# Neighbour words of consecutive nodes, and a block-wide merge in place of the second drain

## The chip, the cores and the metric

The kernel runs on one core of a Trainium2 chip. The metric is device microseconds of that core, as the median of 3 runs. The engines are TensorE (PE in the profile), VectorE (DVE), ScalarE (ACT), GpSimd (POOL) and SyncE (SP), which works off its queue of DMAs here. GpSimd issues all indirect DMAs: gathers and scatters by index.

## The reference

Two layers of a graph network over 4096 nodes with 128 features. The first is attention with 8 heads over the neighbours of each node, the second takes three quantiles, feature by feature, over the kept neighbours. Cut to what matters:

```python
adj = bernoulli(0.0078125, (4096, 4096)); adj = adj | adj.T | eye   # int32
# layer 0
Wh = einsum('nd,hde->hne', nodes, W)
e = leaky_relu(f1[:, :, None] + f2[:, None, :], 0.2)
att = softmax(where(adj > 0, e, -9e15), axis=-1)
h = elu(einsum('hnm,hmd->hnd', att, Wh))
x = layernorm(nodes + elu(cat(h) @ W1 + b1))
# layer 1
mask = adj != 0
keep = mask & ~remove      # remove: one or two neighbours, by rank in the row
svals = sort(where(keep[:, :, None], x[None], big), axis=1)
agg = mean of svals at the 0.25, 0.5 and 0.75 quantile of the kept
out = (0.5 * agg + 0.5 * x) @ W.T + b + x
```

A node has 64.6 neighbours on average, 98 at most.

## The kernel before

Nodes are worked in 32 tiles of 128, a node per partition. The kernel never uses the dense 4096 x 4096 matrix for the layers themselves. A front part (class `Front`) turns each row of adj into a list of up to 104 (`C1`) neighbour numbers, in descending order, -1 or less where there is none. From the lists, `place` finds each node's place among the nodes of its block, ordered by number of neighbours, and scatters the lists there (`rows_d`, line 543, on GpSimd's queue); `keep` makes the shorter list for the second layer. The attention part (`gat`) then gathers the neighbours' rows from DRAM with indirect DMAs (line 975, tile nb). After that comes `sparse`, the second layer, which begins when the first is done.

The tiles are cut into six blocks (`BLOCKS` = 4, 4, 6, 6, 6, 6). `Front.pieces` makes a list of pieces of work: for each block its first drains, second steps, second drains, `place`, and the `keep` of the block before. `gat` works on half tiles, u from 0 to 63. In each step it issues the gathers of half tile u+3 (`load`), multiplies half tile u on TensorE (`rows_sum`: spread, line 1107, on VectorE, then the matmuls into ps_z, line 1115), makes the softmax of u+1 (`probabilities`), copies ps_z out on ScalarE (`collect`, line 1130), moves older tiles on (`combine`), and then takes some pieces of front work:

```python
advance(3 if u < 2 * START[2] else 2)
```

`load` of the first half tile of a block calls `through(b)`, which works off all pieces up to that block's `place`. The row buffers nb are six tiles of 18 gathered rows. A scheduler sets the order of instructions on each engine; each engine works its own in order.

How a list is made, for one tile:

- `scan` loads four quarters of the adj rows (a_i, line 380, on SP's queue). ScalarE makes 0 and 1 in bf16 (nz): once with Relu of the negated value, which sums up negative entries (line 382), once with sign (line 389). TensorE adds 16 column stretches, weighted with 1, 2, 4 ... 2^15 (line 391). The result is 256 words of 16 bits in PSUM (ps_words). Word g holds the nodes g, g + 256, g + 512 and so on. A scan takes two tiles (the first two only one each), in four chunks, with two nz buffers of one chunk.
- `first` makes keys of word times 256 plus g (line 404) and takes the 104 largest by 13 rounds of `drain8`: MAX8 (line 190), and between rounds MATCH_REPLACE8 (line 192), which strikes the eight found ones out.
- `second`, for 2 to 4 tiles at once (`BATCH`), takes the highest bit of each word (`decode`, `peel`) into a candidate number, then drains words with a second bit (24, `C2`), and those with a third (8, `C3`), which are peeled six times (`PEELS`). This leaves 104 + 24 + 48 = 176 candidates in no order (cand).
- `last_` drains the 176 candidates again in 13 rounds into the list, sorted.

Tests that a limit was overflowed go into `spill`; if one was, a flag at the end of the first layer sends the program to a dense version (`general`).

Of the kernel before, what the change touches and what calls it, by code (L numbers as in the profile page):

```python
# [38 lines left out]
F32 = mybir.dt.float32  # L39
# [11 lines left out]
P = 128  # L51
# [19 lines left out]
C3 = 8  # L71
PEELS = 6
CAND = C1 + C2 + C3 * PEELS
# [28 lines left out]
BATCH = 4  # L102
# [83 lines left out]
def drain8(nc, out, work, rounds, gone):  # L186

    for r in range(rounds):
        top = out[:, ts(r, 8)]
        nc.vector.max(out=top, in_=work)  # L190
        if r < rounds - 1:
            nc.vector.match_replace(  # L192
                out=work, in_to_replace=top, in_values=work, imm_value=gone
            )


def peel(nc, pool, wf, base, ids, rest, tag):


    shape = list(wf.shape)  # L200
    e = ids.bitcast(I32)
    nc.vector.tensor_scalar(
        e,
        wf.bitcast(I32),
        23,
        NG1.bit_length() - 1,
        op0=ALU.logical_shift_right,
        op1=ALU.logical_shift_left,
    )
    if rest is not None:  # L210
        pw = pool.tile(shape, I32, name=f"pw_{tag}")
        nc.vector.tensor_scalar(pw, wf.bitcast(I32), 0x7F800000, None, op0=ALU.bitwise_and)
        nc.vector.tensor_sub(rest, wf, pw.bitcast(F32))
    nc.vector.tensor_tensor(ids, e, base, op=ALU.add)


def decode(nc, pool, keys, tag):

    shape = list(keys.shape)
    ki = pool.tile(shape, I32, name=f"ki_{tag}")  # L220
    nc.vector.tensor_copy(ki, keys)
    wi = pool.tile(shape, I32, name=f"wi_{tag}")
    nc.vector.tensor_scalar(wi, ki, NG1.bit_length() - 1, None, op0=ALU.logical_shift_right)
    nc.vector.tensor_scalar(ki, ki, NG1 - 1, None, op0=ALU.bitwise_and)
    wf = pool.tile(shape, F32, name=f"wf_{tag}")
    nc.vector.tensor_copy(wf, wi)
    base = pool.tile(shape, F32, name=f"base_{tag}")
    nc.vector.tensor_scalar(base, ki, -127.0 * NG1, None, op0=ALU.add)
    return wf, base
# [90 lines left out]
class Front:  # L320
# [3 lines left out]
    def __init__(self, tc, nc, c, adj, meta_d, ctx):  # L324
# [11 lines left out]
        self.iota_s = self.iota_g[:, :C1]  # L336
        self.pows = one.tile([P, WBITS, P], BF, name="pows")
# [18 lines left out]
        self.spill = one.tile([P, NT, 5], F32, name="spill")  # L356
# [11 lines left out]
        self.words, self.lists, self.counts = {}, {}, {}  # L368
        self.placed = None

    def scan(self, t, m):

        nc = self.nc
        ps_w = self.psum_w.tile([P, 2, NG1], F32, name="ps_words")
        quarter = N // 4
        for i in range(4):
            nz = self.tp.tile([P, 2, quarter], BF, name="nz", bufs=2)
            for j in range(m):
                a_i = self.tp.tile([P, quarter], I32, name="a_i", bufs=3)
                nc.sync.dma_start(out=a_i, in_=self.adj[ts(t + j, P), ts(i, quarter)])  # L380
                k = 4 * (t + j) + i
                nc.scalar.activation(  # L382
                    nz[:, j, :],
                    a_i,
                    AF.Relu,
                    scale=-1.0,
                    accum_out=self.negative[:, k : k + 1],
                )
                nc.scalar.sign(nz[:, j, :], a_i)
            for b in range(4):  # L390
                nc.tensor.matmul(
                    ps_w[:, :m, :],
                    self.pows[:, 4 * i + b, :],
                    nz[:, :m, ts(b, NG1)],
                    start=i + b == 0,
                    stop=i + b == 6,
                )
        for j in range(m):
            self.words[t + j] = ps_w[:, j, :]

    def first(self, t, k1):
        nc = self.nc
        key = self.tp.tile([P, NG1], F32, name="key")
        nc.vector.scalar_tensor_tensor(
            key, self.words.pop(t), float(NG1), self.iota_g, op0=ALU.mult, op1=ALU.add
        )
        drain8(nc, k1, key, C1 // 8, -1.0)

    def second(self, t, m, k1, cand):

        nc, one = self.nc, self.one
        k1, cand = k1[:, :m], cand[:, :m]
        sp = self.spill[:, t : t + m, :]
        wf, base = decode(nc, one, k1, f"1_{m}")
        rest = one.tile([P, m, C1], F32, name=f"rest1_{m}")
        peel(nc, one, wf, base, cand[:, :, :C1], rest, f"1_{m}")
        nc.vector.tensor_scalar(
            sp[:, :, 0:1], k1[:, :, C1 - 1 :], float(NG1), None, op0=ALU.is_ge
        )
        nc.vector.tensor_scalar(base, base, 127.0 * NG1, None, op0=ALU.add)  # L420
        nc.vector.scalar_tensor_tensor(rest, rest, float(NG1), base, op0=ALU.mult, op1=ALU.add)
        k2 = one.tile([P, m, C2], F32, name=f"k2_{m}")
        for j in range(m):
            drain8(nc, k2[:, j, :], rest[:, j, :], C2 // 8, -1.0)
        nc.vector.tensor_scalar(
            sp[:, :, 1:2], k2[:, :, C2 - 1 :], float(NG1), None, op0=ALU.is_ge
        )
        wf, base = decode(nc, one, k2, f"2_{m}")
        rest = one.tile([P, m, C2], F32, name=f"rest2_{m}")
        peel(nc, one, wf, base, cand[:, :, C1 : C1 + C2], rest, f"2_{m}")  # L430
        nc.vector.tensor_scalar(base, base, 127.0 * NG1, None, op0=ALU.add)
        nc.vector.scalar_tensor_tensor(rest, rest, float(NG1), base, op0=ALU.mult, op1=ALU.add)
        k3 = one.tile([P, m, C3], F32, name=f"k3_{m}")
        for j in range(m):
            drain8(nc, k3[:, j, :], rest[:, j, :], 1, -1.0)
        nc.vector.tensor_scalar(
            sp[:, :, 2:3], k3[:, :, C3 - 1 :], float(NG1), None, op0=ALU.is_ge
        )
        wf, base = decode(nc, one, k3, f"3_{m}")
        for r in range(PEELS):  # L440
            nxt = one.tile([P, m, C3], F32, name=f"rest3_{m}", bufs=2)
            at = C1 + C2 + C3 * r
            peel(nc, one, wf, base, cand[:, :, at : at + C3], nxt, f"3_{m}")
            wf = nxt
        left = one.tile([P, m], F32, name=f"left_{m}")
        nc.vector.reduce_sum(left, wf, axis=AX.X)
        nc.vector.tensor_scalar(sp[:, :, 3:4], left.unsqueeze(2), 0.0, None, op0=ALU.is_gt)

    def place(self, b):
# [5 lines left out]
        work = one.tile([P, max(BLOCKS), C1], F32, name="work")[:, :n, :]  # L455
# [116 lines left out]
    def keep(self, b):  # L572
# [7 lines left out]
        work = one.tile([P, max(BLOCKS), C1], F32, name="work")[:, :n, :]  # L580
# [125 lines left out]
    def pieces(self, order_d, flag_d):  # L706
# [10 lines left out]
        for b, n in enumerate(BLOCKS):  # L717
            lists = self.tp.tile([P, max(BLOCKS), C1], F32, name="lists")

            def open_(b=b, lists=lists):  # L720
                self.lists[b] = lists

            out.append(("open", open_))
            at = START[b]
            while at < START[b] + n:
                m = min(BATCH, START[b] + n - at)
                if n % BATCH:
                    m = n // -(-n // BATCH)
                bufs = {}

                def start(bufs=bufs):
# [1615 lines left out]
```

## Time and profile before

| | |
|---|---|
| median of 3 runs | 7530.93 us |
| lowest, highest | 7525.32, 7533.52 us |
| profiled execution, span | 8384.6 us |
| instructions in it | 31455 |
| granted TensorE clock, mean | 0.547 |
| first gather of the attention part | 142 us |
| 30th of 64 copies out of ps_z | 2219 us |
| last gathers of the attention part | about 3800 us |

The profiled execution's own time is its span of 8384.6 us, 854 us more than the median of the runs; all durations below are from that one execution. A row of a group has the line, engine and operation, output and input tiles, shapes, count, busy time, mean ns of one, and the idle time of that engine just before, with what ended it. "issue" is waiting that the profile puts down to nothing; "remote" is a wait whose release it does not show. One line of the code can stand for several uses, as line 190 for all drains; tile names tell them apart (k from key: first drain; k from rest: the short drains; lists from cand: second drain).

### The profile page before, as it was taken

The numbers are of one execution on the slowest core, as the hardware profiler recorded it, in microseconds if no ns is written. First come the engines' busy times: TensorE is split into PE (matmuls) and PEld (weight loads), VectorE is DVE, ScalarE is ACT, GpSimd is POOL, SyncE is SP. The second block draws the span as 40 slices with busy tenths as digits, with TensorE's granted clock in tenths as the row PEclk, the third lists the DMA queues.
The fourth block names the chain that finished last, engine by engine and source line by source line (L and its number), as shares of the span: only waits on it lengthen the run. The fifth ranks groups of instructions, "written<-read, shape, count | busy, mean of one in ns | idle before, by whom it ended". The sixth has DMA issues, their size and how long they took to land. (4 is left out here: it accounts for less than half of the span.)

```text
span 8384.6 us, 31455 instructions
## 1 busy us (share of the span) xinstructions
PE 1235.7 (15%) x6047; PEld 1032.2 (12%) x6047; DVE 5886.7 (70%) x9454; ACT 2218.9 (26%) x2338; POOL 4358.1 (52%) x4524
## 2 busy tenths in 40 slices
PE   2122222222332332330000000000000000000000
PEld 1121212222231322230000000000000000000000
DVE  6454564454222222224899999999999999999899
ACT  5021121000000000002344443443443433333333
POOL 3545546656666666666455456445554545354410
PEclk5565656565565666565555555555555555555555
DMA  6122222112112111111011111111111111011100
GB/s 192 43 89 71 74 77 64 49 38 50 50 48 50 50 49 50 50 41 39 26 36 35 33 36 43 31 32 38 34 34 31 38 30 35 27 34 32 31 9 1
DMA packets 219060, 380.98 MB, mean 45 GB/s; under 512 B 129283, under 2 KB 129412, under 8 KB 218852
## 3 DMA queue, kind: packets, MB, share of 16 engines
q0 software_dynamic: 145808, 308.58, 13.9%
q1 hardware_dynamic: 72898, 70.23, 2.8%
q14 instruction: 159, 1.30, 0.1%
q8 instruction: 49, 0.80, 0.0%
q10 hardware_dynamic: 146, 0.07, 0.0%
HBM read 368.26 MB, written 10.31 MB: 45 GB/s over the span
## 5 line engine op out<-in xcount | busy, mean ns | idle before, releaser
L1771 DVE TENSOR_TENSOR rows<-low,rows 128x2048 f32<-128x2048 f32 (+10 forms) x1970 | 3649.3, 1893 | 88.0 <-ACT low L1764 61.7
L1726 POOL DMA_INDIRECT rows<-x_d,info x2078 | 2031.9, 978 | 1863.7 <-ACT picked L1826 1184.2
L975 POOL DMA_INDIRECT nb<-xf_d,ids x2190 | 2078.1, 949 | 1329.5 <-issue 625.3
L1764 ACT COPY low<-rows 128x2048 f32<-128x2048 f32 (+8 forms) x985 | 1528.4, 1557 | 2331.8 <-DVE rows L1771 1665.3
L1115 PE MATMUL ps_z<-spread,nb 128*128 128x128 f32 x4500 | 757.9, 325 | 1491.4 <-issue 737.3
L1107 DVE TENSOR_TENSOR spread<-e,ps_small 128x1152 f32<-128x1152 f32 (+4 forms) x312 | 342.2, 1109 | 804.1 <-remote 594.0
L1115 PEld LDWEIGHTS ps_z<-spread,nb 128*128 128x128 f32 x4500 | 702.4, 237 | 1565.9 <-issue 996.7
L1833 PE MATMUL low<-sixth_i,picked 128*128 128x128 f32 x300 | 74.3, 430 | 4347.7 <-ACT low L1764 3413.6
L1833 PEld LDWEIGHTS low<-sixth_i,picked 128*128 128x128 f32 x300 | 65.0, 322 | 4357.0 <-ACT low L1764 3420.9
L1771 DVE TENSOR_TENSOR rows<-low_s,rows 128x512 f32<-128x512 f32 (+3 forms) x798 | 395.3, 523 | 128.7 <-remote 39.9
L1077 ACT ACTIVATE ps_e<-e 128x256 f32<-128x256 f32 (+4 forms) x64 | 26.1, 408 | 1513.9 <-DVE e L1067 556.2
L190 DVE MAX8 k<-key 128x8 f32<-128x256 f32 x416 | 169.0, 416 | 169.6 <-remote 119.5
L1764 ACT COPY low_s<-rows 128x512 f32<-128x512 f32 (+3 forms) x399 | 179.8, 486 | 281.6 <-DVE rows L1771 172.0
L1873 POOL DMA_INDIRECT out<-o,info x32 | 34.9, 1091 | 397.2 <-ACT o L1869 369.3
L1130 ACT COPY zT<-ps_z 128x512 f32<-128x512 f32 x64 | 37.6, 587 | 742.7 <-remote 586.0
L382 ACT ACTIVATE nz<-a_i 128x1024 bf16<-128x1024 int32 x128 | 134.2, 1049 | 328.9 <-remote 198.6
L190 DVE MAX8 lists<-cand 128x8 f32<-128x176 f32 x416 | 128.1, 332 | 69.7 <-remote 47.1
L192 DVE MATCH_REPLACE8 key<-k,key 128x256 f32<-128x256 f32 x384 | 156.1, 408 | 0.0
L1058 DVE TENSOR_TENSOR e<-nb,ps_small 128x64 f32<-128x64 f32 (+9 forms) x200 | 45.2, 237 | 154.4 <-DMA nb<-xf_d,ids 129.9
L1438 DVE SCALAR_TENSOR_TENSOR zT<-zT,ps_h 128x512 f32<-128x512 f32 x64 | 42.0, 682 | 158.0 <-ACT zT L1437 109.7
L1146 PE MATMUL ps_h<-zT,w_ga 128*128 128x256 f32 x256 | 105.3, 569 | 271.3 <-DVE s L1438 157.2
L1775 DVE TENSOR_TENSOR rows<-rows 128x256 f32<-128x256 f32 (+8 forms) x245 | 142.5, 583 | 1.6 <-DVE rows L1771 1.4
(245 smaller groups left out, 2429.0 us busy)
## 6 DMA issues: line engine op xcount, KB each, us to landing
a_i<-in_adj SPq DMA_DIRECT2D x128, 512.0 KB
nb<-xf_d,ids POOLq DMA_INDIRECT x2190
rows<-x_d,info POOLq DMA_INDIRECT x2078
xf_d<-xf POOLq DMA_DIRECT2D x4, 576.0 KB
xf<-in_x POOLq DMA_DIRECT2D x4, 512.0 KB
meta_d<-rowdata_k SPq DMA_DIRECT2D x4, 324.0 KB
abc_ta<-in_L_gnn_a POOLq DMA_DIRECT2D x2, 512.0 KB
w_ga<-in_L_gnn_W POOLq DMA_DIRECT2D x2, 512.0 KB
```

What stands on the lines that cost most here:

```text
L190: nc.vector.max(out=top, in_=work)
L192: nc.vector.match_replace(out=work, in_to_replace=top, in_values=work, imm_value=gone)
L382: nc.scalar.activation(nz[:, j, :], a_i, AF.Relu, scale=-1.0, accum_out=self.negative[:, k : k + 1],)
L975: gather = nc.gpsimd.indirect_dma_start(out=rows[:, used + i, :], out_offset=None, in_=xf_d, in_offset=bass.IndirectOffsetOnAxis(ap=ids[:, ...
L1107: last = nc.vector.tensor_tensor(spread[:, :m], e[:, at : at + m, :].unsqueeze(2).to_broadcast(shape), own.unsqueeze(1).unsqueeze(3).to_br ...
L1115: product = nc.tensor.matmul(ps_z[:, g, :], rows[:, k, :D], spread[:, i].rearrange("p j h -> p (j h)"), start=i0 + i == 0, stop=i0 + i == ...
L1146: nc.tensor.matmul(ps_h[:, k, :], w_sb[:, h0 + k, :], zT[:, h0 + k, :], start=True, stop=True)
L1726: return nc.gpsimd.indirect_dma_start(out=row, out_offset=None, in_=x1_d, in_offset=bass.IndirectOffsetOnAxis(ap=info[:, col : col + 1], a ...
L1764: nc.scalar.copy(packed, lows)
L1771: done = nc.vector.tensor_tensor(to, packed, highs, op=op)
L1775: nc.vector.tensor_tensor(lows, lows, highs, op=ALU.min)
L1833: product = nc.tensor.matmul(made["ps"], v, to, start=i == 0, stop=i == len(found))
```

## The change

A word now holds 16 consecutive nodes, so that the order of words is the order of nodes. The first drain takes keys that are largest for the highest group with a bit in it (group number times 65536 plus the word), 88 at most, in 11 rounds. The highest bit of each, one after the other, is a sorted list already. What is left of words with two or more bits (extras: 24 second bits, 8 words peeled five times) is drained to 24 sorted numbers, and these are merged into the sorted list in a bitonic merge of 128 places, for all tiles of a block in one instruction per half step. The second drain of every tile is gone. To get consecutive nodes, ScalarE writes nz transposed: each quarter is read in order and written with one bit position after the other, 128 elements apart; a scan has two chunks of twice the size, with 32 matmuls of half as many columns. `second` is cut into four pieces per block; `gat` takes 2 and later 1 piece per half tile.

```diff
+WORDS = 88
+PEELS = 5
+EXTRAS = 24
+MERGE = 128
-BATCH = 4
...
     def scan(self, t, m):
...
-        for i in range(4):
-            nz = self.tp.tile([P, 2, quarter], BF, name="nz", bufs=2)
+        for i in range(2):
+            nz = self.tp.tile([P, 2, WBITS, 2 * part], BF, name="nz", bufs=2)
             for j in range(m):
...
+                for q in range(2):
...
+                    to = nz[:, j, :, ts(q, part)].rearrange("p b g -> p g b")
+                    groups = a_i.rearrange("p (g b) -> p g b", b=WBITS)
+                    nc.scalar.activation(
+                        to,
+                        groups,
...
+                    nc.scalar.sign(to, groups)
+            for b in range(WBITS):
                 nc.tensor.matmul(
+                    ps_w[:, :m, ts(i, 2 * part)],
+                    self.pows[:, b, :],
+                    nz[:, :m, b, :],
...
     def first(self, t, k1):
...
+            key, words, 0.0, self.high, op0=ALU.is_gt, op1=ALU.mult
         )
-        drain8(nc, k1, key, C1 // 8, -1.0)
+        nc.vector.tensor_add(key, key, words)
+        drain8(nc, [k1[:, ts(r, 8)] for r in range(WORDS // 8)], key, 0.0)
...
+    def second(self, b, part):
...
+        if part == 3:
+            k4 = one.tile([P, most, EXTRAS], F32, name="k4")[:, :n]
+            for j in range(n):
+                tops = [k4[:, j, ts(r, 8)] for r in reversed(range(EXTRAS // 8))]
+                drain8(nc, tops, self.extra[:, j], -1.0e6)
...
+            for i in range(8):
+                nc.vector.tensor_copy(w[:, :, :, i], v[:, :, :, 7 - i])
+            self.merge(b, up)
+
+    def merge(self, b, up):
...
+        nc.vector.memset(x[:, :, WORDS : MERGE - EXTRAS], -1.0)
+        nc.vector.tensor_tensor(x[:, :, MERGE - EXTRAS :], near, up, op=ALU.min)
+        nc.vector.tensor_tensor(near, near, up, op=ALU.max)
+        step = half // 2
+        while step:
...
+            for i, op in enumerate((ALU.max, ALU.min)):
+                nc.vector.tensor_tensor(ends[i][1], ends[0][0], ends[1][0], op=op)
+            x, y = y, x
+            step //= 2
...
-                    def last_(t=at + j, j=j, b=b, bufs=bufs):
-                        to = self.lists[b][:, t - START[b], :]
-                        drain8(self.nc, to, bufs["cand"][:, j, :], C1 // 8, -1.0e6)
...
+            for part in range(4):
+                out.append((None, lambda b=b, part=part: self.second(b, part)))
...
-            advance(3 if u < 2 * START[2] else 2)
+            advance(2 if u < 2 * START[2] else 1)
```

## The prediction

> **What bounds the kernel now.** I read the page first, then the busy times by stage, then what GpSimd waits for in each stage, then one stall in order of time, then the groups of the instructions that the change touches.
>
> The page's engine row and its 40 slices:
>
> ```profile
> PE 1235.7 (15%) x6047; PEld 1032.2 (12%) x6047; DVE 5886.7 (70%) x9454; ACT 2218.9 (26%) x2338; POOL 4358.1 (52%) x4524
> ...
> DVE  6454564454222222224899999999999999999899
> ...
> POOL 3545546656666666666455456445554545354410
> ```
>
> VectorE at 70% is a mean of two kernels. From slice 20 on (the sorting layer) it is full; the change touches nothing there. In the first 18 slices (the attention layer with the front work folded in) it is half busy, and then a fifth busy. The stages cut at four events: first gather (142 us), the 30th copy out of ps_z (2219 us), the last gathers (3801 us), end. Columns: stretch, its length, PE, PEld, DVE, ACT, POOL busy with instruction counts, granted clock, DMA share, GB/s.
>
> ```profile
> 142.00:2219.00 2077.00, 534.77 (x2686) 441.81 (x2685) 1035.31 (x4315) 269.46 (x433) 1157.30 (x1211) 0.59 0.24 65
> 2219.00:3801.00 1582.00, 490.73 (x2580) 431.21 (x2580) 403.41 (x1028) 89.35 (x167) 1042.03 (x1102) 0.61 0.19 48
> 3801.00:8385.00 4584.00, 159.50 (x592) 130.54 (x591) 4335.70 (x3507) 1769.88 (x1594) 2138.81 (x2176) 0.50 0.11 31
> ```
>
> The first two rows do the same attention work; only the first carries front work besides. By the copies out of ps_z (L1130: the first at 297.9, the 30th at 2219.2, the 62nd at 3800.9 us) a half tile takes 66.2 us with front work (29 steps) and 49.4 us without (32 steps). What GpSimd, which issues every gather, waits for in these two stretches (busy, mean ns | idle before, by releaser):
>
> ```profile
> L975 POOL DMA_INDIRECT nb<-xf_d,ids x1151 | 1096.0, 952 | 826.4 <-PE ps_z L1115 446.9 <-issue 330.9 <-remote 35.1
> ...
> L975 POOL DMA_INDIRECT nb<-xf_d,ids x1040 | 983.1, 945 | 503.4 <-issue 294.7 <-remote 135.5 <-PE ps_z L1115 61.3
> ```
>
> Late, GpSimd issues a gather every 945 ns plus some 0.3 us of its own ("issue"): it is the bound, and waits only 197 us. Early it also waits 447 us for ps_z, that is, for row buffers that PE has not finished with. Adding the waits of its scatters on pos_i (34.3), of me on info (9.1) and of x_d on VectorE (37.8), the early stretch has 563 us of waits. At the late rate (197 us for 1040 gathers) its 1151 gathers would have 218. So **345 us is what front work costs this stretch**. How it costs is seen at 502 to 570 us, where VectorE runs the tail of block 1 in one piece:
>
> ```profile
> 563.12 9.09 PE L1115 MATMUL ps_z<-spread,nb 128*128 128x128 f32 x64 [57.44 <-DVE spread L1107]
> 569.36 0.94 POOL L975 DMA_INDIRECT nb<-xf_d,ids  x1 [45.01 <-PE ps_z L1115]
> ```
>
> The spread of the next half tile stands behind second drains on VectorE; PE idles 57 us for it, the row buffers stay full, and GpSimd stands 45 us.
>
> **The change part by part.** The rows it is costed from:
>
> ```profile
> L190 DVE MAX8 k<-key 128x8 f32<-128x256 f32 x416 | 169.0, 416 | 169.6 <-remote 119.5 <-issue 38.7 <-DVE key L192 5.1
> L192 DVE MATCH_REPLACE8 key<-k,key 128x256 f32<-128x256 f32 x384 | 156.1, 408 | 0.0
> L382 ACT ACTIVATE nz<-a_i 128x1024 bf16<-128x1024 int32 x128 | 134.2, 1049 | 328.9 <-remote 198.6 <-issue 70.1 <-DMA a_i<-in_adj 40.0
> ...
> L190 DVE MAX8 lists<-cand 128x8 f32<-128x176 f32 x416 | 128.1, 332 | 69.7 <-remote 47.1 <-DVE lists L190 7.8 <-issue 7.5
> L192 DVE MATCH_REPLACE8 cand<-lists,cand 128x176 f32<-128x176 f32 x384 | 123.5, 326 | 0.9 <-issue 0.9
> ...
> L391 PE MATMUL ps_words<-nz,pows 128*128 128x512 bf16 x240 | 93.2, 536 | 258.0 <-ACT nz L389 128.0 <-ACT nz L382 65.0 <-issue 35.7
> ...
> L524 DVE TENSOR_SCALAR rowdata<-lists 128x624 int32<-128x624 f32 x4 | 2.9, 714 | 0.0
> ```
>
> *Removed, the second drain.* Per tile 13 MAX8 of 332 ns, 12 MATCH_REPLACE8 of 326 with a value load of 79 each, and a spill test of 140: 4.32 + 4.86 + 0.14 = 9.3 us, times 32 tiles = **298 us** of VectorE.
>
> *First drain, 13 rounds to 11.* Minus 2 x (416 + 408 + 81) ns, plus a tensor_add of 256 with a PSUM input, taken like L404 (411 ns): minus 1.4 us a tile, **minus 45 us**.
>
> *second() by the block, and merge.* From rows of like kind (tensor_tensor 24 wide 173 ns, 312 wide 470, 624 wide 802, so 150 + 1.03 ns an element; MAX8 24 wide 171, 104 wide 256): the old decode, peel and short drains came to 175 us. The new ones: short drains 49, drain of the 64 extras (three MAX8, two MATCH_REPLACE8 a tile) 39, decode and peels 95, reversal copies 8, the merge's 12 steps of 256 or 384 elements per block with its min, max and memset 40: 231 us, **plus 56 us**.
>
> Sum: VectorE loses 287 of some 848 us of this work, and in instructions (a MATCH_REPLACE8 counted with its value load) 3248 become 2010. The idle time in front of the drains (169.6 + 69.7 + 71.9 + 30.8 us in the rows of both drains, mostly "remote" waits of 2 to 3 us) shrinks with the number, not on top of what follows.
>
> *Moved.* Pieces per half tile go from 3 and 2 to 2 and 1. I counted, in the order in which both kernels' instructions stand on VectorE, the front work between one softmax and the next, each at the durations above: before 798 us over 29 half tiles (27.5 each; longest run without an attention instruction 43 us), after 551 us over 39 (14.1 each; longest 23 us). Attention itself needs 12.1 us of VectorE a half tile. The scatters of rows (L543) and own rows (L951) on GpSimd's queue, the index loads and the 128 loads of a_i on SP's keep their numbers; the scatters of a block come later in the schedule, but each block's last piece still stands 3 or more half tiles ahead of its first gather. What lies past step 29 is not free any more: ten half tiles that had no front work get about 8 us each.
>
> *What of it is on the path.* Start: VectorE runs from 21.5 to 132.6 us almost without a gap, and the first scatter waits for it. The second drain of block 0 takes 94.8 to 122.2 there (27 us); about 12 us of extras and merge replace it, the first drains give back 5: **minus 20 us**, less what the new scan costs the first words. Stretch 142 to 2219: if every microsecond of front work costs alike, 551/798 of 345 stays, 238 us, a gain of 107. If a half tile hides about 12 us (late, VectorE is busy 403 of 1582 us, so there is room), the work above that falls from 454 to 156 us and 119 us stays, a gain of **226 us**. I take the second, because the waits come in pieces of 10 to 58 us behind long runs and not evenly.
>
> *Scan on PE.* The matmuls double to 544 with half the columns. The row of 512 columns is 536 ns, that of 256 columns 371: 100 us becomes about 197, plus 34 of weight loads, spread over half tiles in which PE is busy a quarter of the time. About one part in six on the path: plus 20 us. If PE's cover were gone, 130. In return nz holds a whole scan in its two buffers where it held half, so ACT waits less for PE; I count nothing for it.
>
> *Scan on ACT.* The 256 activations write 2-byte elements 256 bytes apart. No row shows such a write. The nearest, L524, reads every 32 bytes on VectorE and takes 714 ns for 624 elements, less than a contiguous tensor_tensor of that size (802): no penalty. [...] I take 25, nearer to the row.
>
> [...]
>
> Sum: -20 - 226 + 20 + 25 = -201 us in the profiled execution. That one is 8384.6 us long, the median 7530.93. The sorting layer alone is 4336 us of VectorE work, so at least 600 of the 854 us lie in the first layer; 0.3 us of "issue" on 2190 gathers would be 650. Without it GpSimd is less of a bound there and VectorE more, which speaks for the gain, while all waits shrink, which speaks against. I carry it over one to one: **7330 us**.
>
> **The rivals.** (A) As above, gain 100 to 340 us, 7190 to 7430.
>
> (B) The waits are latency (gather, softmax, spread, PE) and not VectorE time: only the start gains, 7500. For it: spread also waits 435 us on "remote" between 2000 and 3700 us. Against it: the 57 us wait above, and that the pace rises with front work.
>
> (C) ACT's strided write becomes the bound, and the kernel is slower. Place: ACT's queue, where two logits steps and one zT copy of each half tile stand behind scan pairs. At four element times the scan costs 256 x 2.6 = 655 us more, ACT is over half busy until 1650 us, every softmax step waits about half a pair of 7 us, three times in 30 half tiles: +330, and +60 at the start. Less the gain of 246: about 7675. It decides from about three element times, where the loss equals the gain. [...] Against it: L524.
>
> (D) A node overflows the smaller limits and the flag sends the kernel to the dense path. Counted on the given adjacency: at most 85 non-empty words of consecutive nodes (88 is the limit), 19 words with a second bit (24), 4 with a third (8), 5 bits in a word, 20 extras (24). No flag; I give it nothing.
>
> **How the numbers follow.** 0.2% is 15 us, about what a measurement of this kernel can tell from no change. A 0.62, B 0.13 (of which 0.02 within 15 us), C 0.21, a balance of gain and loss within 15 us 0.04. Faster 0.73, same 0.06, slower 0.21. The range goes from 7160 (A with the idle time in front of the drains on top) to 7545 (B and the balance); A's own is 7190 to 7430.
>
> **What would show it.** First scatter near 113 us instead of 133; 352 MAX8 of 256, none on cand; 30 ps_z copies by about 2000 us; GpSimd's early wait on ps_z down from 447 to about 200 us; the last stretch unchanged at 4580. ACT's scan rows at 1.05 us speak for A, above 3 us for C. A wait on ps_z above 400 us with fewer drains would refute the step from VectorE's work to GpSimd's waits.

## The result, and the profile after

The changed kernel takes **7911.8 us** (median of 4, 7910.35 to 7912.58) against 7530.8 before: a ratio of **1.0504**, interval 1.0492 to 1.0517. The forecast was 7330. One thing is needed to read the numbers below: in this study every run of a session lay at one of two levels, before at 7525 to 7531 us ("the level 7525") or at 8354 to 8379 us ("the level 8370"; one chip showed both in different sessions), so each result is given as a ratio to before in its own session, and times are compared within a level. The profile that the forecast used is of the level 8370, its times are of the level 7525.

The page of the changed kernel (level 7525, span 7909.9), engine row and slices:

```profile
PE 1076.7 (14%) x6319; PEld 955.9 (12%) x6319; DVE 5618.9 (71%) x8217; ACT 3133.4 (40%) x2338; POOL 4385.1 (55%) x4524
...
DVE  2243544445433323249999999999999999999999
ACT  9988675600000000014444433434434344343433
POOL 0066755777777777777545455455645455454500
```

ScalarE has gone from 2218.9 to 3133.4 us and is full in the first slices; GpSimd stands still in the first two, where it was busy before. The groups of the scan's activations (busy, mean ns | idle before):

```profile
L365 ACT ACTIVATE nz<-a_i 128x1024 bf16<-128x1024 int32 x128 | 626.4, 4998 | 23.9 <-PE ps_words L374 20.9 <-DMA a_i<-in_adj 3.0
L372 ACT ACTIVATE nz<-a_i 128x1024 bf16<-128x1024 int32 x128 | 610.3, 4873 | 2.0
L365 ACT ACTIVATION_READ_ACCUMULATOR nz<-a_i 128x1 f32 x128 | 63.7, 498 | 0.0
```

5.0 and 4.9 us where before had 1.05 (rows L382 and L389), and the readout after each Relu 498 ns instead of 187 (L382 of before: 23.9 us for 128). The scan has 1237 us of activations instead of 265. The other work in ScalarE's queue shows it. In order of time, from 176 us on:

```profile
176.79 4.74 ACT L372 ACTIVATE nz<-a_i 128x1024 bf16<-128x1024 int32 x1
181.04 0.92 ACT L244 COPY xf<-ps_fa 128x512 f32<-128x512 f32 x1
181.86 4.74 ACT L372 ACTIVATE nz<-a_i 128x1024 bf16<-128x1024 int32 x1
186.11 5.04 ACT L365 ACTIVATE nz<-a_i 128x1024 bf16<-128x1024 int32 x1
```

One copy of the table xf, between scans, at 181 us; GpSimd's store of that table waits for it. What GpSimd waits for in the whole profile (us in total, times, longest):

```profile
POOL nb L999 <- issue: 646.3, 2121, 0.3
...
POOL rows_d L591 <- DVE pos_i L568: 174.6, 1, 174.6
POOL nb L999 <- PE ps_z L1139: 173.9, 18, 43.9
POOL xf_d L246 <- ACT xf L244: 172.7, 1, 172.7
```

The first scatter (L591) comes at 374.1 us instead of 133.0, and the first gather at 388.3 instead of 142.2. Cut at the first and the last gather (stretch, length, PE, PEld, DVE, ACT, POOL busy with counts, granted clock, DMA share, GB/s):

```profile
0.00:388.30 388.30, 55.17 (x290) 42.57 (x290) 89.30 (x481) 383.75 (x151) 20.18 (x37) 0.59 0.26 78
388.30:3429.00 3040.70, 846.92 (x5330) 768.32 (x5330) 1183.29 (x4193) 974.51 (x588) 2174.57 (x2277) 0.62 0.29 68
3429.00:7910.00 4481.00, 174.58 (x699) 145.03 (x699) 4346.27 (x3543) 1775.13 (x1600) 2190.32 (x2211) 0.50 0.13 32
```

Until the first gather ScalarE is busy 383.75 of 388.30 us: it sets the start.

### The profile page after: what moved, and what is told of

Read it like the earlier page. It is cut to its first block, busy times and chain, and to the rows that moved or that the text cites. A ratio compares the mean times of both kernels' runs of the same rounds, so it can differ in the third digit from the quotient of the medians.

```text
span 7909.9 us, 30720 instructions
## 1 busy us (share of the span) xinstructions
PE 1076.7 (14%) x6319; PEld 955.9 (12%) x6319; DVE 5618.9 (71%) x8217; ACT 3133.4 (40%) x2338; POOL 4385.1 (55%) x4524
## 5 line engine op out<-in xcount | busy, mean ns | idle before, releaser
L1139 PE MATMUL ps_z<-spread,nb 128*128 128x128 f32 x4500 | 599.3, 299 | 1154.8 <-DVE spread L1131 1154.8
L1139 PEld LDWEIGHTS ps_z<-spread,nb 128*128 128x128 f32 x4500 | 586.5, 214 | 1176.7 <-DVE spread L1131 647.4
L1101 ACT ACTIVATE ps_e<-e 128x256 f32<-128x256 f32 (+4 forms) x64 | 30.3, 474 | 1610.9 <-DVE e L1082 871.0
L365 ACT ACTIVATE nz<-a_i 128x1024 bf16<-128x1024 int32 x128 | 626.4, 4998 | 23.9 <-PE ps_words L374 20.9
L372 ACT ACTIVATE nz<-a_i 128x1024 bf16<-128x1024 int32 x128 | 610.3, 4873 | 2.0
L1102 DVE TENSOR_TENSOR ps_e<-e,ps_e 128x256 f32<-128x256 f32 (+4 forms) x64 | 28.9, 452 | 281.0 <-ACT ps_e L1101 281.0
L374 PE MATMUL ps_words<-nz,pows 128*128 128x256 bf16 (+1 forms) x544 | 100.6, 363 | 439.0 <-ACT nz L372 272.8
L190 DVE MAX8 k<-key 128x8 f32<-128x256 f32 x352 | 141.6, 420 | 0.7
L1801 DVE TENSOR_TENSOR rows<-rows 128x128 f32<-128x128 f32 (+7 forms) x231 | 141.0, 613 | 0.2
L591 POOL DMA_INDIRECT rows_d<-rowdata,pos_i x32 | 31.4, 982 | 184.0 <-DVE pos_i L568 174.6
```

What stands on the lines that cost most here:

```text
L365: nc.scalar.activation(to, groups, AF.Relu, scale=-1.0, accum_out=self.negative[:, k : k + 1],)
L372: nc.scalar.sign(to, groups)
L1139: product = nc.tensor.matmul(ps_z[:, g, :], rows[:, k, :D], spread[:, i].rearrange("p j h -> p (j h)"), start=i0 + i == 0, stop=i0 + i == ...
L1801: nc.vector.tensor_tensor(highs, lows, highs, op=ALU.max)
```

## The experiments

The theory: ScalarE's 2-byte write, 256 bytes apart, is the loss. There are two rivals for the loss: the doubled matmuls, and the slower pace of the pieces. A second question is whether less VectorE work gains anything, as the forecast had it. Results in one table (levels and medians in us; "pace" is the number of pieces that `advance` takes a half tile, early and late; "in order" means that ScalarE writes nz as it reads; variants of the changed kernel have its pace, 2/1, where nothing else is said; gathers from the profiles):

| kernel | level | median | ratio to before [95%] | first, last gather |
|---|---|---|---|---|
| after_2 (the changed kernel again, pace 2/1) | 7525 | 7905.8 | 1.0506 [1.0489, 1.0524] | 388.1, 3426.1 |
| a_flat_32 (in order, pace 3/2) | 7525 | 7516.2 | 0.9988 [0.9982, 0.9995] | 136.9, 3037.5 |
| b_21 (before, pace 2/1) | 7525 | 7555.3 | 1.0041 [1.0027, 1.0055] | 142.0, 3073.7 |
| b_3 (before, pace 3/2) | 8370 | 8383.8 (one) | | 142.2, 3735.9 |
| a_flat (in order, 2/1) | 8370 | 8217.5 | 0.9811 [0.9794, 0.9827] | 136.0, 3569.7 |
| a_flat_2 (the same again) | 8370 | 8219.6 | 0.9806 [0.9789, 0.9822] | 136.9, 3583.5 |
| a_read (stride on the read) | 8370 | 8268.9 | 0.9874 [0.9858, 0.9891] | 175.6, 3617.0 |
| a_half (half the strided writes) | 8370 | 8321.7 | 0.9941 [0.9924, 0.9958] | 214.9, 3667.5 |
| a_early (8 tiles in order) | 8370 | 8413.1 | 1.0038 [1.0023, 1.0052] | 187.6, 3766.4 |
| a_12 (12 tiles in order) | 8370 | 8323.2 | 0.9967 [0.9957, 0.9977] | 137.2, 3694.8 |
| a_more (in order, work put back, 3/2) | 8370 | 8481.1 | 1.0121 [1.0104, 1.0138] | 137.2, 3829.0 |
| a_more_21 (the same, 2/1) | 8370 | 8325.4 | 0.9968 [0.9955, 0.9980] | 135.4, 3677.8 |
| after_32 (changed, pace 3/2) | 8370 | 8790.0 | 1.0534 [1.0516, 1.0551] | 387.9, 4126.5 |

**The write in order.** ScalarE writes nz as it reads a_i; the stride goes to TensorE's moving operand (32 bytes).

```diff
-nz = self.tp.tile([P, 2, WBITS, 2 * part], BF, name="nz", bufs=2)
+nz = self.tp.tile([P, 2, 2 * part, WBITS], BF, name="nz", bufs=2)
-to = nz[:, j, :, ts(q, part)].rearrange("p b g -> p g b")
+to = nz[:, j, ts(q, part), :]
-    nz[:, :m, b, :],
+    nz[:, :m, :, b],
```

> The changed kernel with nz laid out by group and then by bit: ACT writes its 1024 elements next to each other, and the matmul reads its moving operand every 16th element (32 bytes apart). All else is the changed kernel. Theory 1 (ACT's strided write is the whole loss): the scan's activations fall from 4.94 to about 1.05 us, the first scatter comes at 110 to 145 us instead of 374, and the time is 7250 to 7450. Theory 2 (other parts lose too: 544 matmuls instead of 272, a piece or two of front work a half tile, the block's batch): ACT's rows fall just so, but the time stays above 7600. Theory 3: the stride only moves to PE: the rows of 256 columns go from 0.36 to over 0.8 us, and the time ends between.

It landed on the level 8370: 0.9811. At 7525 it ran with 3 and 2 pieces:

```diff
-advance(2 if u < 2 * START[2] else 1)
+advance(3 if u < 2 * START[2] else 2)
```

> The changed kernel with ACT writing in order (PE reads with the stride), and besides with 3 and 2 pieces of front work a half tile instead of 2 and 1, as before. Theory 1 (the fewer, longer pieces are what the schedule can hide one or two at a time): slower than with 2 and 1, by 30 to 100 us. Theory 2 (front work is bound by ACT and SP ahead of it, and more pieces a half tile bring the late blocks forward at no cost): the same within 20 us or faster. The range where before takes 7531: 7250 to 7450; where it takes 8377: 8200 to 8320.

Groups of a_flat_32:

```profile
L374 PE MATMUL ps_words<-nz,pows 128*128 128x256 bf16 x480 | 224.8, 638 | 115.7 <-ACT nz L372 71.5 <-DVE key L391 36.5 <-DVE most_r L1044 3.9
...
L365 ACT ACTIVATE nz<-a_i 128x1024 bf16<-128x1024 int32 x128 | 134.4, 1050 | 215.2 <-DMA a_i<-in_adj 133.8 <-PE ps_words L374 80.7
```

ScalarE is at 1050 ns; a matmul takes TensorE 638 ns with the stride where the changed kernel has 371. The time is 7516: **the loss of 390 us is gone, and what is left of the gain is 9 us**. This kernel differs from the changed one in the pace as well; that the pace alone does not take the loss away is shown at the level 8370, by a_flat (the changed kernel's pace, in order: 0.9811) and after_32 (this pace, the stride kept: 1.0534). Its stretches, against those of the changed kernel above:

```profile
0.00:136.90 136.90, 88.25 (x276) 42.24 (x277) 89.28 (x481) 93.69 (x149) 20.10 (x37) 1.00 0.69 220
136.90:3037.50 2900.60, 966.00 (x5346) 778.34 (x5344) 1210.29 (x4193) 353.71 (x590) 2173.78 (x2277) 0.63 0.30 71
3037.50:7518.00 4480.50, 174.53 (x699) 145.25 (x699) 4345.84 (x3543) 1772.78 (x1600) 2186.33 (x2211) 0.50 0.13 32
```

The loss splits into 388.3 - 136.9 = **251 us before the first gather** and 3040.7 - 2900.6 = **140 us between gathers**; the rest is equal (4481.0 and 4480.5). What GpSimd waits for in a_flat_32, until 3450 us:

```profile
POOL nb L999 <- issue: 647.0, 2123, 0.3
...
POOL xf_d L246 <- ACT xf L244: 59.5, 1, 59.5
...
POOL rows_d L591 <- DVE pos_i L568: 39.4, 1, 39.4
POOL nb L999 <- PE ps_z L1139: 16.7, 9, 9.8
```

Waits on ps_z are 16.7 us where the changed kernel has 173.9: that difference, 157, covers the 140. It comes from the softmax. Its first step on ScalarE scales the logits (L1101), and VectorE (L1102) waits for that step, first in the changed kernel and then in a_flat_32:

```profile
DVE ps_e L1102 <- ACT ps_e L1101: 281.0, 33, 45.6
DVE ps_e L1102 <- ACT ps_e L1101: 19.3, 37, 0.6
```

The longest of these waits in the changed kernel, in ScalarE's order of time, then VectorE's instruction that waited:

```profile
502.48 9.57 ACT L372 ACTIVATE nz<-a_i 128x1024 bf16<-128x1024 int32 x2
511.56 0.74 ACT L1101 ACTIVATE ps_e<-e 128x232 f32<-128x232 f32 x1
512.34 0.40 DVE L1102 TENSOR_TENSOR ps_e<-e,ps_e 128x232 f32<-128x232 f32 x1 [45.60 <-ACT ps_e L1101]
```

A step of 0.7 us came last in a row of scan activations that filled ScalarE for those 45 us. As for GpSimd, 2277 instructions at 0.955 us plus 0.30 of issue are 2857 of the 2900.6 us: in a_flat_32 the stretch stands on GpSimd's issue.

**The pace, on the kernel before.** `advance(2 ... else 1)` in before.

> The kernel before with 2 and 1 pieces of front work a half tile instead of 3 and 2, and no other change. Its pieces are smaller and more in number (per four tiles four first drains, one decode, four second drains), so its front work lasts 1.5 to 2 times as many half tiles. Theory 1 (the spread is the gain): faster than before by 30 to 120 us. Theory 2 (the last blocks come too late for their gathers): slower, by more than 100 us.

Slower by 30 us: neither theory. It waits 50.1 us for ps_z, and its stretch between gathers is 2931.7 us. Before itself has no profile at this level; with b_21's start (142.0) and end (4480) taken for it, an estimate for its stretch is 7525 - 4622 = about 2903 us, that of a_flat_32. By this estimate the 287 us less VectorE work moved the stretch by 2 us.

**The changed kernel and the one in order again.**

> The changed kernel, unchanged. Before has two levels here, 7531 where the change was measured and 8377 beside the first four runs, while the busy times of the engines are the same. Theory 1: whatever sets the level adds to both kernels alike; where before takes 8377 the changed kernel takes about 8377 x 1.05 = 8800. Theory 2: the slow level is waiting (1240 to 1290 us of idle time in front of the gathers against 845), so added ACT time hides in it; where before takes 8377 the changed kernel takes 8377 plus at most 60, since the one with half of the strided writes took 8322 and the one with none 8218, 104 us for half.

At 7525 the ratio repeats. So it did, with that of a_flat_32, in one more session of that level: 1.0505 [1.0488, 1.0523] for the changed kernel, 0.9989 [0.9982, 0.9996] for the one in order.

> The changed kernel, unchanged, to be had at the level at which before takes about 8370 (with 3 and 2 pieces a half tile it took 8790 there, 1.053 of before). In order with its own pace it took 8220 there; with the first twelve tiles in order 8323, and with the first eight 8413 (first gather at 188 instead of 137). Theory 1 (the late first gather adds its 251 us whole, and the later writes about 100): 8220 + 251 + 100 = 8570, 1.02 of before. Theory 2 (the late start is made up by waits that front work made before): under 8450. Theory 3 (pace is of no account): 8790. Where before takes 7525: 7906, as before.

> The changed kernel with ACT writing in order at 3 and 2 pieces a half tile, to be had at the level at which before takes about 8370; with 2 and 1 it took 8220 there, and with the second drain's work put back 8325 (2 and 1) and 8481 (3 and 2). Theory 1 (the pace costs, whatever the work): 8220 + 156 = 8376, no gain on before at all. Theory 2 (the pace costs only what the put-back work makes of it): 8220 to 8280. Where before takes 7525: 7516 again.

**The stride on ScalarE's read.** `to = nz[:, j, :, ts(q, part)]` and `groups = a_i.rearrange("p (g b) -> p b g", b=WBITS)`: reads of 4 bytes, 64 apart, writes in runs of 128 bytes.

> The changed kernel with the stride on ACT's other side: the activation reads a_i every 16th 4-byte element (64 bytes apart) and writes runs of 64 elements (128 bytes) in order; PE reads as in the changed kernel. Theory 1 (it is the scattered 2-byte write that costs): the activations take 1.05 to 1.3 us and the time is that of the kernel with stride on PE, 7250 to 7450. Theory 2 (any stride on ACT costs, reading as writing): the activations stay near 5 us, and the time near 7900.

1.92 us an activation, between the theories; the first gather is at 175.6 us, and the kernel 51 us slower than with the stride on TensorE. A strided read costs ScalarE too, 0.87 us an activation where the write costs 3.9.

**Half of the strided writes.** Both Relus of a half row come first and write in order into nz, which both signs then overwrite with the stride.

```diff
+plain = nz[:, j].rearrange("p b g -> p (b g)")
-nc.scalar.activation(to, groups, AF.Relu, scale=-1.0, ...)
+nc.scalar.activation(plain[:, ts(q, quarter)], a_i, AF.Relu, scale=-1.0, ...)
```

> The changed kernel with only half of the strided writes: the Relu, whose output is not used, writes 1024 elements next to each other into the same nz (both Relus of a half row before both signs); only the sign writes every 256 bytes. ACT loses 128 x 3.9 = 500 us of about 990 us added. Theory 1 (the strided write is the loss, and most of it where ACT is full, before the first gather): the first scatter comes at about 240 us instead of 374 and the time is about halfway between the changed kernel and the one that writes in order, 7580 to 7720. Theory 2 (other parts lose): over 7800.

Groups of a_half, then its first scatter in order of time:

```profile
L376 ACT ACTIVATE nz<-a_i 128x1024 bf16<-128x1024 int32 x128 | 597.2, 4885 | 1.3
...
L365 ACT ACTIVATE nz<-a_i 128x1024 bf16<-128x1024 int32 x128 | 148.1, 1160 | 166.7 <-remote 138.2 <-issue 18.7 <-DMA a_i<-in_adj 7.0
```

```profile
204.31 1.04 POOL L595 DMA_INDIRECT rows_d<-rowdata,pos_i  x1 [126.42 <-DVE pos_i L572]
```

Half of the writes, but only 79 of 251 us of late first gather (214.9 - 136.0). Until its first gather ScalarE is busy 206.7 us here, 165.4 in a_read, 383.8 in the changed kernel and 93.8 in a_flat. So 113, 72 and 290 us of added work make the gather 79, 40 and 251 us late: ScalarE's slack covers 32 to 39 us, and all that comes on top is delay (in a_early, below, the slack covers less: 63 us of added work make 51 of delay). The expected times were for the level 7525; at 8370 the row says 104 us more than in order.

**Where in the kernel the write costs.** In order for `t < 8`, then for `t < 12`, strided for the rest.

> The changed kernel, with ACT writing in order (and PE reading with the stride) for the first eight tiles only; the other 24 are written 256 bytes apart. In the changed kernel the first gather comes at 388 us (137 with all tiles in order), and after it GpSimd waits 175 us for ps_z (17 with all in order). Theory 1 (both count): first gather at about 137, GpSimd still waits 150 to 220 us for ps_z, 7640 to 7720 where before takes 7525. Theory 2 (only the start counts: the late waits are the start's backlog, front work and attention crowding after a late start): waits under 60, 7510 to 7560. Theory 3 (the ACT queue is as full as before, now beside attention): 7750 to 7900.

> The changed kernel with ACT writing in order (and PE reading with the stride) for the first twelve tiles, and writing 256 bytes apart for the other 20. With eight tiles in order the first gather came at 187.6 us, since ACT scans ahead of the first block's end, and the time was 8413 where before takes 8378. Theory 1 (start and later scans both cost): first gather at 137 to 150; 8340 to 8420 where before takes 8378; 7590 to 7680 where it takes 7525 (20/32 of the 158 us of waits on ps_z that the changed kernel has more than the one in order, and little of the 251 us of the start). Theory 2 (only the start counts): 8220 to 8300, or 7510 to 7540 with waits under 60 us.

Eight tiles are too few: ScalarE scans ahead of block 0's end, so the first gather is still 51 us late. With twelve the start is right (137.2), and the pace is that of a_flat_2 (0.9806), so what remains is the price of later strided writes alone: 0.9967 / 0.9806 is 1.6%, about 135 us for 20 tiles. GpSimd's waits in a_12, and VectorE's for the scaled logits:

```profile
POOL nb L1003 <- PE ps_z L1143: 518.9, 28, 59.4
...
POOL rows_d L595 <- DVE pos_i L572: 39.6, 1, 39.6
...
DVE ps_e L1106 <- ACT ps_e L1105: 154.7, 17, 46.9
```

a_flat_2 has 377.8 us on ps_z and 8.6 on the scaled logits: the writes make the softmax, and with it ps_z, late. So both shares of the loss are the write's. The size of the second at the level 7525, 140 us, was measured only with the pace changed as well. The repeat of the kernel in order:

> The changed kernel with ACT writing in order and PE reading with the stride, with the changed kernel's 2 and 1 pieces of front work a half tile. With 3 and 2 pieces it took 7516 where before takes 7525. Theory 1 (every gather waits for GpSimd's own issue there, so when front work is done is of no account): 7510 to 7530, and the whole of the 390 us between this and the changed kernel is the write. Theory 2 (the slower pace costs, as 30 us in the kernel before): 7540 to 7600. Where before takes 8377: 8218 again.

It gave the level 8370 once more, so the two paces of the in-order kernel were never timed at one level.

**VectorE's work put back.** The kernel in order, and in it, for the 28 tiles after block 0, 13 rounds of drain that nothing uses, as many as the change removed:

```diff
+if t >= START[1]:
+    more = self.tp.tile([P, C1], F32, name="more")
+    drain8(nc, [more[:, ts(r, 8)] for r in range(C1 // 8)], key[:, :176], -1.0)
```

> The changed kernel with ACT writing in order and 3 and 2 pieces a half tile (7516), and with as much VectorE work put back as the change removed: for the 28 tiles after the first block, 13 MAX8 and 12 MATCH_REPLACE8 of 176 elements on the used-up keys, into a tile that nothing reads; 9.3 us a tile, 257 us in all. Theory 1 (VectorE's front work lies on the path of the attention layer, as the forecast had it, about 0.75 us a us): 190 us slower, about 7700. Theory 2 (at the level of 7525 it is hidden under GpSimd's issue): 7515 to 7545, with under 50 us of waits on ps_z. Where before takes 8377, theory 2 says that it costs 80 to 200 us there.

> The changed kernel with ACT writing in order and the second drain's VectorE work put back on 28 tiles (257 us, in a tile that nothing reads), at 2 and 1 pieces a half tile. At 3 and 2 pieces it took 8481 where before takes 8378, against 8220 in order without it at 2 and 1. Theory 1 (front work on VectorE is on the path where the level is 8378, and hidden under GpSimd's issue where it is 7525): 8378 gives 8400 to 8480, and 7525 gives 7515 to 7550 with under 60 us of waits on ps_z in front of the gathers. Theory 2 (the pace made the 261 us, not the work): 8220 to 8280 at the first level. Theory 3 (the work is on the path at both levels): about 7700 at the second.

At 8370 the 257 us cost 0.9968 / 0.9806 = 1.65%, about 136 us, at pace 2/1: VectorE's work is on the path there, about 0.53 us of time for each us of work. At pace 3/2 the kernel is slower by another 1.0121 / 0.9968 = 1.5%, about 128 us. Neither ran at 7525, so the put-back itself is not tested there; that VectorE's work is covered at 7525 rests on a_flat_32.

**The changed kernel at the other level.**

> The changed kernel with its strided write kept and 3 and 2 pieces of front work a half tile instead of 2 and 1: against the one that writes in order at that pace (7516 where before takes 7525) it differs in the side of the stride alone. Theory 1 (the write is the whole loss, and the pace of the pieces is of no account): 7890 to 7930, as the changed kernel. Theory 2 (the pace brings front work earlier, into the time in which ACT is full): 7950 to 8100. Where before takes 8377, no run of the changed kernel is there yet: those with half of the writes (8322) and with eight tiles in order (8413) put it at 8420 to 8520, 1.005 to 1.017 of before.

1.0534: the loss against before is 436 us there, at pace 3/2, well above the 1.005 to 1.017 expected. At its own pace the changed kernel was not had at 8370; how much of this is the pace stays open.

**What the level is.** Three more profiles of before, all at 8370:

> The kernel before, unchanged, profiled once more. The profile shown of it spans 8384.6 us where its median is 7531, with 594 us of waits of spread on 'remote' and 586 of the zT copies; the changed kernel's profile (7909.9) has none of these. Theory 1: those waits are of that one execution only; a new profile spans about 7530, its sorting stage about 4443 (that of the changed kernel) instead of 4584, first gather at about 130 us, and so the attention stage is about 2960 us long. Theory 2: profiling always costs this kernel 850 us: span above 8300 again.

> The kernel before, for its profile at the level of its median. Where before takes 8377 its profile has PE waiting 640 to 740 us for nothing that is seen ('issue') in front of the ps_z matmuls; where it takes 7525 no profile of it was seen yet. Theory 1 (at 7525 PE has its instructions in time, and GpSimd's issue of a gather, 0.95 + 0.30 us, bounds the whole attention layer): no 'issue' on PE, under 60 us of waits on ps_z in front of the gathers, first gather 142, last gather at about 3050. Theory 2 (front work on VectorE costs at this level too): 200 us or more of waits on ps_z.

> The kernel before, for its profile at the level of 7525, of which there is none yet. Theory 1 (there PE has its instructions in time, and GpSimd's 0.95 + 0.30 us a gather bounds the whole attention layer): no 'issue' in front of the ps_z matmuls, under 60 us of waits on ps_z in front of the gathers, last gather at about 3050. Theory 2 (front work on VectorE costs there too): 200 us or more of waits on ps_z.

So it is not the profiling: the medians of before in those sessions are 8354 to 8379 as well. What TensorE waits for in the profile that the forecast was made from:

```profile
PE ps_z L1115 <- issue: 737.3, 372, 43.7
...
PE ps_z L1115 <- DVE spread L1107: 625.0, 55, 58.2
```

and in b_21, at 7525, where no row with "issue" stands before ps_z:

```profile
PE ps_z L1115 <- DVE spread L1107: 782.0, 55, 46.1
```

TensorE's weight loads in b_3, in order of time:

```profile
2727.14 5.16 PEld L1115 LDWEIGHTS ps_z<-spread,nb 128*128 128x128 f32 x44
2734.94 0.19 PEld L1115 LDWEIGHTS ps_z<-spread,nb 128*128 128x128 f32 x1 [2.64 <-issue]
2737.06 0.29 PEld L1115 LDWEIGHTS ps_z<-spread,nb 128*128 128x128 f32 x1 [1.93 <-issue]
```

44 loads in 5 us, then one every 2 to 3 us (so on to 2744.80), with nothing seen that they wait for. In these stretches TensorE, not VectorE, holds the row buffers. What holds TensorE itself up is not shown by these traces. The sorting layer is about 165 us longer at this level as well (4643 to 4647 us after the last gather, in every kernel, against 4480).

**The price of a stride, by itself.** 20 conversions of one a_i tile (1024 int32) into 1024 bf16, twice each, put ahead of the changed kernel's first scan (shortened):

```diff
+def far(n):   return flat.rearrange("p (b g) -> p g b", g=n)     # write, 2n bytes apart
+def near(n):  return from_.rearrange("p (g b) -> p g b", b=quarter // n)
+def skip(n):  return from_.rearrange("p (b g) -> p g b", g=n)    # read, 4n bytes apart
+def fill(n):  return flat.rearrange("p (g b) -> p g b", b=quarter // n)
+nc.scalar.sign(flat, from_)                # L373
+nc.scalar.sign(far(2), near(2))            # L374; L375 to L379: far(4), 8, 16, 64, 256
+nc.scalar.sign(fill(2), skip(2))           # L380; L381: fill(4)
+nc.vector.tensor_copy(flat, from_)         # L386; L387, L388: far(2), far(8)
+nc.vector.tensor_copy(fill(2), skip(2))    # L390; L391: fill(8)
```

> The changed kernel with 13 sign activations and 7 tensor_copy's, twice each, put ahead of its first scan, which turn one a_i tile of 1024 integers into 1024 bf16 in one nz tile, which nothing reads, with the output strided by 4 to 512 bytes and a read in order, or the input strided by 8 to 1024 bytes and a write in order. Known of ACT: 1.05 us in order, 4.9 us with writes 256 bytes apart, 1.9 us with reads 64 bytes apart and runs of 128 bytes written. [...] Theory 2 (any write that is not next to the last costs the same): 4.9 from 4 bytes on. VectorE: theory 1 of the same rows on both engines; theory 2 VectorE, whose strided read of 32 bytes cost nothing in the profile before, takes the same at all strides.

```profile
L376 ACT ACTIVATE nz<-a_i 128x1024 bf16<-128x1024 int32 x2 | 10.0, 5018 | 0.0
...
L377 ACT ACTIVATE nz<-a_i 128x1024 bf16<-128x1024 int32 x2 | 9.4, 4689 | 0.0
L375 ACT ACTIVATE nz<-a_i 128x1024 bf16<-128x1024 int32 x2 | 5.2, 2598 | 0.0
...
L388 DVE CAST nz<-a_i 128x1024 bf16<-128x1024 int32 x2 | 4.9, 2473 | 0.0
...
L381 ACT ACTIVATE nz<-a_i 128x1024 bf16<-128x1024 int32 x2 | 4.1, 2071 | 0.0
...
L374 ACT ACTIVATE nz<-a_i 128x1024 bf16<-128x1024 int32 x2 | 3.2, 1619 | 0.0
L380 ACT ACTIVATE nz<-a_i 128x1024 bf16<-128x1024 int32 x2 | 2.7, 1372 | 0.0
L373 ACT ACTIVATE nz<-a_i 128x1024 bf16<-128x1024 int32 x2 | 2.4, 1191 | 2.8 <-DMA a_i<-in_adj 2.8
L391 DVE CAST nz<-a_i 128x1024 bf16<-128x1024 int32 x2 | 2.2, 1098 | 0.0
...
L386 DVE CAST nz<-a_i 128x1024 bf16<-128x1024 int32 x2 | 1.4, 694 | 56.7 <-ACT nz L385 56.7
L390 DVE CAST nz<-a_i 128x1024 bf16<-128x1024 int32 x2 | 1.4, 694 | 0.1
```

ScalarE's writes: in order 1191 ns, 4 bytes apart 1619, 8 bytes 2598, 16 bytes 5018 or 4689 (L376 is 16 bytes, L377 32), and no more beyond: 128 and 512 bytes apart take 4.9 us both. The price rises with the distance up to 16 bytes and is level from there, so theory 2 (4.9 us from 4 bytes on) is wrong. It is not cheap below that, though: 1.4 times the price in order at 4 bytes, 2.2 times at 8. Counted in stretches of these 16 bytes that the 1024 writes step into (1024, 512 and 256 of them at 16, 8 and 4 bytes), it is 4.9, 5.1 and 6.3 ns a stretch; so an estimate for the writes that dominate is 5 ns a stretch. Reads: 1372 at 8 bytes, 2071 at 16, and level from there. VectorE: a write 16 bytes apart 2473 against 694, a read 32 bytes apart 1098 against 694.

## Why the prediction was wrong, point by point

**The step that failed: "Scan on ACT".** No run shows its term of 25 us, which was the author's estimate, "nearer to the row"; in its place the runs showed 251 us at the start and 140 between gathers (the latter with the pace of the pieces in it). The row L524 was the wrong nearest row, in three ways: a read, not a write; on VectorE, not ScalarE; of 4-byte elements, not 2. And it did not even show "no penalty". It was compared with a tensor_tensor (802 ns), but the profile of before has a tensor_scalar on as many elements, read in order:

```profile
L462 DVE TENSOR_SCALAR work<-lists 128x624 f32<-128x624 f32 x4 | 1.9, 479 | 0.0
```

L524's 714 ns are 1.5 times that, near the ratio of L391 to L386 (1.6). That L524 writes int32 is not the reason: a cast to int32 of that size (L615) takes 478 ns. On ScalarE the write takes 4.7 times what it takes in order (4.94 us against 1.05).

**The place was mis-sized too.** The forecast counted nothing of the write's cost on the start but a remark. But before the first gather there is no attention to hide under: ScalarE has the scans of ten tiles (42 Relus) in its queue ahead of the first gather; with its other work that is 383.75 us, where it had 90 before. "Minus 20 us" at the start was plus 246. With the write in order it was minus 5 to 6 (142.2 to 136.9): the lists of block 0 do come 16 us sooner after its first drains (26 us in a_flat_32, 43 before), but these end 8 us later (87.6 against 79.5 us), where the forecast had them 5 us sooner, and `place` takes 3 us longer. Why the drains end later was not tested.

**Rival C was the right mechanism,** at 0.21. Its place (ScalarE's queue) and its sign held; its 655 us of ScalarE (256 x 2.6 is 666; the four element times were an assumption, which no row of before shows) were 972 (1237 - 265), its "+60 at the start" was 251, its "+330" after it (its terms make 315) was 140, and its "less the gain of 246" was about 9. Its sign, scan rows above 3 us, is what the profile shows.

**"I carry it over one to one" failed.** At the level of the profile the gain without the write is real: between gathers 3446.6 us in a_flat_2 against 3593.7 in b_3, 147 us, where the forecast's terms (226, less 20 for TensorE) say 206; put-back work costs 0.53 us a us there against the forecast's 226 / 287, which is 0.79. At the level of the times the kernel in order gains 9 us, 5 to 6 of them at the start. That is rival B's number (7500 against 7516), but not B's reason: the stretch is full of GpSimd's own issue. The page shown held the warning: 854 us between the profiled execution and the median, and 737 us of "issue" in front of the ps_z matmuls (372 waits). The forecast put the 854 us down to 0.3 us of "issue" per gather; but that row is 646 us in the changed kernel's profile too, whose span is its median. It was the "issue" of TensorE that belonged to the level. So did the 4580 us expected of the last stretch: before's last gather is at 3739.1 us (3801 is the 62nd copy out of ps_z), and the 4645 us after it are 4481 in the changed kernel and 4480 in b_21, which has before's work.

**What held:** 352 MAX8 on key and none on cand (DVE instructions 9454 to 8217); no dense path; no price of the doubled matmuls that shows between gathers at 7525 (a_flat_32 has them, at 638 ns, and stands on GpSimd's issue); gathers of about the same length (954 ns each in the changed kernel, 949 before); A's mechanism at the level where it was read. "Wait on ps_z down from 447 to about 200" came out as 173.9, but for another reason: in b_21, which has before's work, it is 50.1 at that level.

## What to carry to other kernels

Before trusting a layout that lets one engine read in order because another writes with a stride, price the writer by a row of that engine writing, and if there is none, by one measured for it, as in the run rows (20 conversions of one tile, where the write 16 bytes apart took 5018 ns against 1191 in order); then ask which stage has nothing to hide it, which here was the start. When the profiled execution and the median differ by a tenth, as here, a gain read from the one need not carry over to the other: look first for the wait that explains the difference. The version in order, with the stride on TensorE's moving operand and 3 and 2 pieces a half tile, is the fastest of those timed at 7525, by 0.1% of before; with 2 and 1 pieces it gains 1.9% at 8370.

## What the runs showed of the hardware

- ScalarE writing 1024 bf16 from int32: 1.05 to 1.19 us in order, 1.6 at 4 bytes apart, 2.6 at 8, 4.7 to 5.0 from 16 on. A read of int32: 1.4 at 8 bytes, 2.0 to 2.1 from 16 on, and 1.9 in a_read. The readout of the accumulator behind a strided activation is 498 ns instead of 187.
- VectorE's cast: a write 16 bytes apart 3.6 times (2473 against 694), a read 32 bytes apart 1.6 times.
- TensorE with a bf16 moving operand 32 bytes apart: 638 ns for 256 columns in a_flat_32, against 371 in order in the changed kernel and in before.
- Two levels, 11% apart, for the same program, by session; in the profiles before, b_3 and b_4 at the slower one TensorE stands 737.3, 776.4 and 720.6 us in front of ps_z for nothing that the trace shows.
